# Moving the preparations of the edge messages ahead of the turned pass, and tile-wise waits for all pools, in a graph network kernel

## The chip, the cores and the metric

The kernel runs on one core of a Trainium2 chip. The core has five engines with a queue each: TensorE (PE, matmuls), VectorE (DVE), ScalarE (ACT), GpSimd (POOL) and SyncE (SP, which only issues transfers). Each works through its own instructions in a fixed order and waits for the others by semaphores. Transfers are issued by SP and ACT, and by POOL for indirect ones (gathers by an index), and run on 16 DMA engines. The metric is the device time of one execution in microseconds; three runs of the kernel before gave a median of 4243.05 us.

## The reference

There are 6,250 nodes with 64 features, 206,250 edges sorted by destination, and 64 features for each edge. Four layers follow each other, each on the normalised nodes and added to them:

```python
h = jnp.maximum(_layernorm(x, axis=-1), 0.0)
x = x + _L0_gnn_ref(h, edge_index, ...)   # two normalised sums over neighbours, W3, relu, W4
h = jnp.maximum(_layernorm(x, axis=-1), 0.0)
x = x + _L1_gnn_ref(h, edge_index)        # one sum, rows and columns exchanged
h = jnp.maximum(_layernorm(x, axis=-1), 0.0)
x = x + _L2_gnn_ref(h, edge_attr_64, ...) # messages, see below
h = jnp.maximum(_layernorm(x, axis=-1), 0.0)
x = x + _L3_gnn_ref(edge_index, h)        # three sums, averaged
```

The third one:

```python
Vp = leaky_relu(V @ pAw + pAb, 0.2) @ pBw + pBb
x = relu(relu(E @ mlp_w1 + mlp_b1) @ mlp_w2 + mlp_b2)
msg = sigmoid(x @ Bw + Bb) * Vp[src] + (x @ Cw + Cb)
M = clip(msg, 1e-5, None) ** 2
mean = segment_sum(M, dst, n) / maximum(cnt, 1.0)[:, None]
return mean ** 0.5
```

## The kernel before

The function `fast` does all of it; a second one, `general`, stands in a conditional block that is entered only if `fast` finds its assumptions on the edges broken, which these inputs don't do.

*Stages.* The nodes are padded to 49 blocks of 128, in 7 chunks of 7 blocks. The adjacency matrix A is built first, in 14 strips of 448 columns, in bf16, each written to device memory (L928 to L962); the first sum runs beside it, and its tail, `hidden`, makes V3. Then come two gathers (`gather`, L972): each multiplies all of A with the nodes, three bf16 parts of each value, strip by strip. A strip is loaded by SP in 7 pieces of 784 KB from a pool `apool` of 16 buffers, so there are 98 pieces to a gather, and one piece is 21 matmuls. After every second strip a function of chunk c runs: `convolved(c)` in the first gather, which ends in U3, the input of the second; `turned(c)` in the second (L1017), the turned pass. `turned(c)` adds to X, takes the layer norm (`normed`: DVE operations, ACT's square root at L695, DVE again), transposes on PE, multiplies by pAw, applies the leaky step `aT` on DVE (L1029), multiplies by pBw, adds the bias and stores the chunk of Vp to device memory (L1036).

*The messages.* Edges go in 202 groups of 1,024. For each group POOL issues 8 indirect fetches of rows of Vp (`fetched`, L1235, line 1238), SP loads the edge features, and PE, ACT and DVE work on groups in a pipeline written out by hand (`slot`, L1312, under `manual_schedule`). The fetch needs all 7 chunks of Vp and the indices src_g; v has 4 buffers. Beside the groups, slots take on part of the last layer's first sum and the comparison of A with its transpose (`some_of`).

*The preparations.* Before the first slot, L1050 to L1114 make what the slots need: weights on a diagonal (in the pool `const`, loaded at the start of the program), BC, the biases in three bf16 parts (a chain of five DVE operations and three small transfers on SP, BC_b), the index tables src_g and dst_g (one transfer of 808 KB each on SP, in runs of 8 integers of 4 bytes), a check that each edge lies in its window (`origin`, 194 memsets on POOL; `rel`, `off`, `missed` on DVE), `lane`, `own`, `count`. Those that are used later lie in the pool cpool, those used only here in tpool, which is closed at L1114, and mpool of the slots comes on its bytes.

*Order and memory.* Outside `slot` the order of the instructions on each engine is chosen when the program is built, by a scheduler that takes what is ready in its own model of time, earlier lines first; on the chip that order is kept. Pools are laid out as a stack from the lower end of SBUF. A pool that opens on the bytes of closed ones waits: all its tiles wait for every user of these pools. The same holds for PSUM. In the compiled program SP's and ACT's transfers share eight completion semaphores in turn, and a transfer waits for the one that had its semaphore before.

Of the kernel before, what the change touches and what calls it, by code (L numbers as in the profile page):

```python
# [8 lines left out]
F32 = mybir.dt.float32  # L9
# [9 lines left out]
D = 64  # L19
# [596 lines left out]
def fast(ctx, tc, bad, x, src, dst, edge_attr, W3, b3, W4, b4, w1, b1, w2, b2, Bw, Bb, Cw, Cb,  # L616
# [40 lines left out]
            nc.scalar.dma_start(t[k * D:(k + 1) * D, k * D:(k + 1) * D], m)  # L657
        return t

    node = ctx.enter_context(tc.tile_pool(name="node", bufs=1))  # L660
    stat = ctx.enter_context(tc.tile_pool(name="stat", bufs=2))
    deg_dst = const.tile([P, NB], F32, name="deg_dst")
    missed = const.tile([P, 3], F32, name="missed")

    def blocks(c):
        return slice(c * CB, (c + 1) * CB)

    def over_features(v, n=CB):
        return v.unsqueeze(2).to_broadcast([P, n, D])

    def over_blocks(v, n):
        return v.unsqueeze(1).to_broadcast([P, n, D])
# [71 lines left out]

    X = node.tile([P, NB, D], F32, name="X")
    nc.scalar.dma_start(X, x.rearrange("(b p) f -> p b f", p=P))
    early = ExitStack()
    early_pool = early.enter_context(tc.tile_pool(name="early_pool", bufs=1))
    with ExitStack() as ph:

        ipool = ph.enter_context(tc.tile_pool(name="ipool", bufs=1))
        with ExitStack() as first:
            dpool = first.enter_context(tc.tile_pool(name="dpool", bufs=1))
            dst_i = dpool.tile([P, K1], I32, name="dst_i")
            nc.sync.dma_start(dst_i, dst.rearrange("(p k) -> p k", p=P))
            src_i = dpool.tile([P, K1], I32, name="src_i")
# [31 lines left out]
        exact_i = ipool.tile([P, GC], I32, name="exact_i")  # L788
        junk = ipool.tile([P, P], F32, name="junk")
        looked = ExitStack()  # L790
        npool = looked.enter_context(tc.tile_pool(name="npool", bufs=1))
        near = npool.tile([P, NS], F32, name="near")
        nc.sync.dma_start(near, looks.partition_broadcast(P))
        for c in range(GC):
# [5 lines left out]
        looked.close()  # L800


        rpool = ph.enter_context(tc.tile_pool(name="rpool", bufs=3))
        opool = ph.enter_context(tc.tile_pool(name="opool", bufs=2))
        spool = ph.enter_context(tc.tile_pool(name="spool", bufs=2))
        wpool = ph.enter_context(tc.tile_pool(name="wpool", bufs=1))

        key = ipool.tile([P, 2, GC * P], BF16, name="key")
        below = ipool.tile([P, 3, GC], F32, name="below")
# [9 lines left out]

        with ExitStack() as ps:  # L820
            first = ExitStack()
            psum = first.enter_context(tc.tile_pool(name="ps_", bufs=1, space=PSUM))
            p = psum.tile([P, 512], F32, name="p_node")
            nc.tensor.transpose(p[:D, :P], W3_sb, ident)
            nc.vector.tensor_copy(W3T, p[:D, :P])
# [47 lines left out]
            nc.tensor.transpose(p[:, :NB], by_block, ident[:NB, :NB])  # L873
            nc.vector.tensor_copy(deg_dst, p[:, :NB])
            first.close()
            psum = ps.enter_context(tc.tile_pool(name="ps0", bufs=1, space=PSUM))
            norm0 = inverse_root(deg_dst, 1, "norm0")
            norm3 = inverse_root(deg_dst, 0, "norm3")

# [107 lines left out]


    with ExitStack() as ph:
        wpool = ph.enter_context(tc.tile_pool(name="wpool", bufs=2))  # L990
        U3 = of_nodes(node)
        with tc.tile_pool(name="apool", bufs=16) as apool, \
                tc.tile_pool(name="ps1", bufs=1, space=PSUM) as psum:

            def convolved(c, y):
                z = wpool.tile([P, CB, D], F32, name="z")
                nc.scalar.activation(z, y, AF.Copy)
                add_whole(z, V3, c)
                nc.vector.tensor_mul(z, z, over_features(norm0[:, blocks(c)]))
                nc.vector.tensor_add(z, z, over_blocks(b4_r, CB))  # L1000
                nc.vector.tensor_add(X[:, blocks(c), :], X[:, blocks(c), :], z)
                h = wpool.tile([P, CB, D], F32, name="h")
                normed_and_split(h, U3, c, norm3)

            gather(apool, wpool, psum, V3, convolved)

        pAw_sb = wpool.tile([D, D], F32, name="pAw_sb")
        nc.scalar.dma_start(pAw_sb, pAw)
        pBw_sb = wpool.tile([D, D], F32, name="pBw_sb")
        nc.scalar.dma_start(pBw_sb, pBw)  # L1010
        pAb_c = column(pAb, 1, "pAb_c")
        pBb_r = rows(pBb, "pBb_r")

        with tc.tile_pool(name="apool", bufs=16) as apool, \
                tc.tile_pool(name="ps2", bufs=1, space=PSUM) as psum:

            def turned(c, y):  # L1017
                z = wpool.tile([P, CB, D], F32, name="z")
                nc.vector.tensor_mul(z, y, over_features(norm3[:, blocks(c)]))
                nc.vector.tensor_add(X[:, blocks(c), :], X[:, blocks(c), :], z)  # L1020
                h = wpool.tile([P, CB, D], F32, name="h")
                normed(h, X[:, blocks(c), :])
                hT = to_features(wpool, psum, h)
                aT = wpool.tile([D, W], F32, name="aT")
                for lo, hi in ((0, 512), (512, W)):
                    p_a = psum.tile([D, 512], F32, name="p_a", bufs=2)
                    nc.tensor.matmul(p_a[:, :hi - lo], pAw_sb, hT[:, lo:hi], start=True, stop=True)
                    nc.scalar.activation(aT[:, lo:hi], p_a[:, :hi - lo], AF.Identity, bias=pAb_c)
                nc.vector.scalar_tensor_tensor(aT, aT, 0.2, aT, op0=OP.mult, op1=OP.max)  # L1029
                p_v = psum.tile([P, CB, D], F32, name="p_v", bufs=2)  # L1030
                for k in range(CB):
                    nc.tensor.matmul(p_v[:, k, :], aT[:, k * P:(k + 1) * P], pBw_sb,
                                     start=True, stop=True)
                v = wpool.tile([P, CB, D], F32, name="v")
                nc.vector.tensor_add(v, p_v, over_blocks(pBb_r, CB))
                nc.sync.dma_start(  # L1036
                    Vp_dram[c * W:(c + 1) * W, :].rearrange("(b p) f -> p b f", p=P), v)

            gather(apool, wpool, psum, U3, turned)


    early.close()
    late = ctx.enter_context(tc.tile_pool(name="late", bufs=1))
    H = late.tile([P, NB, D], F32, name="H")
    U3 = of_nodes(node)
    part = ctx.enter_context(tc.tile_pool(name="part", bufs=1))
    Y = part.tile([P, CS, CW], F32, name="Y")
    piece_pool = ctx.enter_context(tc.tile_pool(name="piece_pool", bufs=3))
    with ExitStack() as ph:
        cpool = ph.enter_context(tc.tile_pool(name="cpool", bufs=1))  # L1050
        before = ExitStack()
        tpool = before.enter_context(tc.tile_pool(name="tpool", bufs=1))
        w1_d = diagonal(w1, "w1_d")
        w2_d = diagonal(w2, "w2_d")
        b1_c = column(b1, 2, "b1_c")
# [56 lines left out]
                       allow_small_or_imprecise_dtypes=True)  # L1112

        before.close()  # L1114
        mpool = ph.enter_context(tc.tile_pool(name="mpool", bufs=3))
        ps_a = ph.enter_context(tc.tile_pool(name="ps_a", bufs=1, space=PSUM))
        n1 = stat.tile([P, NB], F32, name="n1")
        nc.vector.tensor_scalar_max(n1, deg_dst, 1.0)
        nc.vector.reciprocal(n1, n1)
# [255 lines left out]
        nc.vector.tensor_add(of_all[:, 0:1], of_all[:, 0:1], of_all[:, 2:3])  # L1375
        nc.vector.tensor_copy(bad, of_all[0:1, 0:1])


    with ExitStack() as ph:
        apool = ph.enter_context(tc.tile_pool(name="apool", bufs=12))  # L1380
        wpool = ph.enter_context(tc.tile_pool(name="wpool", bufs=2))
        psum = ph.enter_context(tc.tile_pool(name="ps4", bufs=1, space=PSUM))
        upool = ph.enter_context(tc.tile_pool(name="upool", bufs=1))

        for layer in range(3):
            V3 = of_nodes((upool, node)[layer]) if layer < 2 else None
# [77 lines left out]
```

## Time and profile before

| what | value |
|---|---|
| runs, median (lowest to highest) | 4243.05 us (4241.24 to 4245.13) |
| the profiled execution | 3727.58 us |
| its span | 3725.9 us |
| PE busy | 3092.7 us (83%) |
| POOL busy | 1666.7 us (45%) |
| DVE busy | 1890.3 us (51%) |
| ACT busy | 1282.9 us (34%) |
| read and written in device memory | 562.82 and 83.58 MB |
| first gather's first matmul | 614.14 us |
| second gather's first piece issued | 830.74 us |
| last matmul of the second gather ends | 1082.52 us |
| first fetch of the messages | 1128.00 us |

The profiled execution is 515 us shorter than the median of the runs without a profile; the trace shows only the former. Times in the profile count from the start of the span. A row of the timeline gives start, duration, engine, line, operation, output and inputs, and in brackets how long the engine had been idle and what ended that wait. `SPq`, `ACTq` and `POOLq` are the issue of transfers on these engines.

### The profile page before, as it was taken

The numbers are of one execution on the slowest core, as the hardware profiler recorded it, in microseconds if no ns is written. First come the engines' busy times: TensorE is split into PE (matmuls) and PEld (weight loads), VectorE is DVE, ScalarE is ACT, GpSimd is POOL, SyncE is SP. The second block draws the span as 40 slices with busy tenths as digits, with TensorE's granted clock in tenths as the row PEclk, the third lists the DMA queues.
The fourth block names the chain that finished last, engine by engine and source line by source line (L and its number), as shares of the span: only waits on it lengthen the run. The fifth ranks groups of instructions, "written<-read, shape, count | busy, mean of one in ns | idle before, by whom it ended". The sixth has DMA issues, their size and how long they took to land.

```text
span 3725.9 us, 57673 instructions
## 1 busy us (share of the span) xinstructions
PE 3092.7 (83%) x23299; PEld 1853.5 (50%) x23299; DVE 1890.3 (51%) x3525; ACT 1282.9 (34%) x2108; POOL 1666.7 (45%) x1870
## 2 busy tenths in 40 slices
PE   0499998999967777888878788787888887799999
PEld 0366665555544444444444444454444444466665
DVE  5999992221214555555655655555555565530100
ACT  0477772001103334433433443443443443210000
POOL 4100000000006777777777777777777777400000
PEclk9999998999987887888888888888888888899999
DMA  3244445968894333344344334334333433499997
GB/s 108 82 183 183 182 184 245 421 270 334 332 188 142 87 88 83 104 110 129 87 119 121 103 104 119 105 102 119 103 108 107 129 104 99 147 350 376 355 357 310
DMA packets 278027, 650.35 MB, mean 175 GB/s; under 512 B 106506, under 2 KB 158788, under 8 KB 275700
## 3 DMA queue, kind: packets, MB, share of 16 engines
q1 hardware_dynamic: 220036, 584.91, 43.4%
q0 software_dynamic: 54112, 58.92, 8.1%
q8 instruction: 185, 3.03, 0.3%
q10 hardware_dynamic: 3600, 2.73, 0.3%
q14 instruction: 94, 0.76, 0.1%
HBM read 562.82 MB, written 83.58 MB: 173 GB/s over the span
## 4 chain that ended last, share of the span: by engine, by line
PE 35%; POOL 32%; issue 14%; DMA 9%; DVE 8%; ACT 2%; POOLq 0%; DVEq 0%; ACTq 0%; SPq 0%
POOL v L1238 32%; PE p_sum L742 26%; DMA v<-Vp_dram,src_g 6%; PE p_a L944 3%; PE p_node L733 2%; DVE hd L935 1%; DVE lo L935 1%; PE p_bc L1264 1%; DMA dst_g<-in_dst 1%; DMA piece<-A 1%; DVE m L1273 0%; DVE m L1274 0%; PE p_node L915 0%; DVE junk L849 0%; PE p_node L725 0%
## 5 line engine op out<-in xcount | busy, mean ns | idle before, releaser
L1238 POOL DMA_INDIRECT v<-Vp_dram,src_g x1616 | 1606.2, 994 | 529.1 <-issue 460.8
L742 PE MATMUL p_sum<-piece,U 128*64 128x448 bf16 x10290 | 1051.7, 360 | 20.0 <-issue 9.9
L742 PEld LDWEIGHTS <-U 128*64 128x64 bf16 x12348 | 694.9, 111 | 527.5 <-issue 95.5
L1264 PE MATMUL p_bc<-BC,h 128*128 128x256 f32 x1616 | 603.6, 509 | 0.0
L1273 DVE TENSOR_TENSOR m<-gate,v 128x512 f32<-128x512 f32 x202 | 140.0, 693 | 798.1 <-DMA v<-Vp_dram,src_g 567.5
L1260 PE MATMUL p_bc<-BC_b,ones 3*128 3x512 bf16 x404 | 182.0, 450 | 359.4 <-DVE m L1274 358.8
L1280 ACT ACTIVATE m<-m 128x512 bf16<-128x512 f32 x202 | 127.3, 630 | 990.7 <-DVE m L1275 990.7
L1090 POOL MEMSET origin<- 128x1 f32 (+1 forms) x194 | 6.5, 96 | 970.8 <-PE p_sum L742 970.8
L1264 PEld LDWEIGHTS p_bc<-BC,h 128*128 128x128 f32 x1616 | 349.7, 240 | 157.6 <-issue 117.1
L1260 PEld LDWEIGHTS <-ones 3*128 3x128 bf16 x404 | 37.5, 93 | 613.6 <-DVE m L1274 486.2
L948 ACT ACTIVATE strip<-p_a 128x784 bf16<-128x784 f32 x392 | 301.7, 820 | 90.0 <-PE p_a L944 88.6
L1250 PE MATMUL p<-h,w_d 128*128 128x512 f32 x404 | 222.6, 633 | 50.7 <-ACT h L1254 50.7
L983 ACT ACTIVATE y<-p_sum 128x448 f32<-128x448 f32 x56 | 30.4, 543 | 678.1 <-PE p_sum L742 678.1
L1254 ACT ACTIVATE h<-p,b_c 128x512 f32<-128x512 f32 x404 | 255.0, 684 | 3.5 <-PE p L1250 3.4
L935 DVE TENSOR_TENSOR lo<-count,key 128x2048 bf16<-128x2048 bf16 x196 | 239.7, 1223 | 0.0
L742 PE MATMUL p_sum<-strip,U 128*64 128x448 bf16 x2058 | 236.2, 358 | 0.4 <-ACT strip L948 0.4
L1156 DVE SCALAR_TENSOR_TENSOR junk<-p_sum,there 128x896 bf16<-128x896 bf16 x196 | 212.3, 1083 | 12.1 <-PE p_e L1246 9.9
L944 PE MATMUL p_a<-hd,lo 128*128 128x98 bf16 x3136 | 189.5, 214 | 33.3 <-DVE lo L935 31.9
L1250 PE MATMUL p<-eT,w_d 128*128 128x512 f32 x404 | 212.3, 608 | 0.0
L944 PEld LDWEIGHTS <-lo 128*128 128x128 bf16 x3136 | 160.0, 101 | 103.4 <-DVE lo L935 81.5
L1391 DVE TENSOR_TENSOR z<-p_node,norm 128x448 f32<-128x448 f32 x21 | 13.1, 625 | 390.3 <-PE p_node L733 390.3
L1292 PE MATMUL p_s<-m,to 128*128 128x192 bf16 x1616 | 202.7, 278 | 1.1 <-DVE r_s L1300 0.4
(177 smaller groups left out, 3191.8 us busy)
## 6 DMA issues: line engine op xcount, KB each, us to landing
piece<-A SPq DMA_DIRECT2D x498, 784.0 KB, 8.7
A<-strip SPq DMA_DIRECT2D x14, 5488.0 KB, 16.5
e<-in_edge_attr SPq DMA_DIRECT2D x202, 256.0 KB, 2.8
v<-Vp_dram,src_g POOLq DMA_INDIRECT x1616
there<-A SPq DMA_DIRECT2D x56, 448.0 KB, 3.9
there<-A SPq DMA_DIRECT2D x56, 336.0 KB, 5.2
pairs<-pair SPq DMA_DIRECT2D x1, 1616.0 KB
Vp_dram<-v SPq DMA_DIRECT2D x7, 224.0 KB, 2.3
```

Of the source, the lines that this page charges most:

```text
L742: nc.tensor.matmul(p[half * D:(half + 1) * D, :w], U3[:, b, k, :], at_block, start=(i < 2), stop=(i >= 3 * n - 2))
L935: nc.vector.tensor_tensor(t, of.unsqueeze(1).to_broadcast(t.shape), key[:, k, at:at + GB].rearrange("p (h j) -> p h j", j=GQ) .unsqueeze(2 ...
L944: nc.tensor.matmul(p[:, j, :2 * NB], lo[:, g // GQ, :, g % GQ], hd[:, g // GQ, :, g % GQ], start=True, stop=True)
L948: nc.scalar.activation(strip[:, :, col:col + 2 * SG].rearrange("p b (j l) -> p b j l", l=2), p[:, :, :2 * NB].rearrange("p j (b l) -> p b ...
L1156: nc.vector.scalar_tensor_tensor(junk, p.rearrange("p a q -> p (a q)"), 0.0, there, op0=OP.add, op1=OP.not_equal, accum_out=unlike[:, n:n ...
L1238: nc.gpsimd.indirect_dma_start(out=v[:, j, :], out_offset=None, in_=Vp_dram[:, :], in_offset=bass.IndirectOffsetOnAxis(ap=src_g[:, g, j:j ...
L1250: nc.tensor.matmul(of[g][p], w, of[g].pop(x), start=True, stop=True)
L1254: nc.scalar.activation(of[g][t], of[g].pop(p), **how)
L1260: nc.tensor.matmul(p_bc[:, 4 * b:4 * b + 4].rearrange("p j o f -> p (j o f)"), ones, BC_b, start=True, stop=False)
L1264: nc.tensor.matmul(p_bc[:, 2 * q:2 * q + 2].rearrange("p j o f -> p (j o f)"), h2[:, q * P:(q + 1) * P], BC, start=False, stop=(k == 1))
L1273: nc.vector.tensor_mul(m, of[g].pop("gate"), of[g].pop("v"))
L1292: nc.tensor.matmul(p, to[:, :, j], m3[:, j].rearrange("p t f -> p (t f)"), start=(j == 0), stop=(j == J - 1))
```

## The change

All pools of `fast` get `reuse_waits="tile"`: a tile that comes on bytes of released pools waits only for the users of earlier tiles on its own bytes (in PSUM, on its own bank), not for all users of these pools. The preparations of the messages, unaltered in themselves, stand ahead of the turned pass's `apool` and PSUM pool instead of after the pass. cpool and tpool are opened with `side="right"`, at the upper end of SBUF; tpool is closed before the turned pass's `apool` opens, cpool after the messages. That `apool` has 14 buffers for 16.

```diff
-    node = ctx.enter_context(tc.tile_pool(name="node", bufs=1))
-    stat = ctx.enter_context(tc.tile_pool(name="stat", bufs=2))
+    node = ctx.enter_context(tc.tile_pool(name="node", bufs=1, reuse_waits="tile"))
+    stat = ctx.enter_context(tc.tile_pool(name="stat", bufs=2, reuse_waits="tile"))
...
+    apart = ctx.enter_context(ExitStack())
     early = ExitStack()
-    early_pool = early.enter_context(tc.tile_pool(name="early_pool", bufs=1))
+    early_pool = early.enter_context(tc.tile_pool(name="early_pool", bufs=1, reuse_waits="tile"))
...
         pBb_r = rows(pBb, "pBb_r")
 
-        with tc.tile_pool(name="apool", bufs=16) as apool, \
-                tc.tile_pool(name="ps2", bufs=1, space=PSUM) as psum:
+        cpool = apart.enter_context(tc.tile_pool(name="cpool", bufs=1, side="right", reuse_waits="tile"))
+        before = ExitStack()
+        tpool = before.enter_context(tc.tile_pool(name="tpool", bufs=1, side="right", reuse_waits="tile"))
+        w1_d = diagonal(w1, "w1_d")
...
+        BC = cpool.tile([P, 4 * D], F32, name="BC")
+        nc.vector.memset(BC, 0.0)
...
+        src_g = cpool.tile([P, G, J], I32, name="src_g")
+        nc.sync.dma_start(src_g, src.rearrange("(g p j) -> p g j", p=P, j=J))
+        dst_g = tpool.tile([P, G, J], I32, name="dst_g")
+        nc.sync.dma_start(dst_g, dst.rearrange("(g p j) -> p g j", p=P, j=J))
...
+        count = cpool.tile([P, P, J], BF16, name="count")
...
+        before.close()
+
+
+        with tc.tile_pool(name="apool", bufs=14, reuse_waits="tile") as apool, \
+                tc.tile_pool(name="ps2", bufs=1, space=PSUM, reuse_waits="tile") as psum:
...
     with ExitStack() as ph:
-        cpool = ph.enter_context(tc.tile_pool(name="cpool", bufs=1))
-        before = ExitStack()
-        tpool = before.enter_context(tc.tile_pool(name="tpool", bufs=1))
-        w1_d = diagonal(w1, "w1_d")
...
-        before.close()
-        mpool = ph.enter_context(tc.tile_pool(name="mpool", bufs=3))
-        ps_a = ph.enter_context(tc.tile_pool(name="ps_a", bufs=1, space=PSUM))
+        mpool = ph.enter_context(tc.tile_pool(name="mpool", bufs=3, reuse_waits="tile"))
+        ps_a = ph.enter_context(tc.tile_pool(name="ps_a", bufs=1, space=PSUM, reuse_waits="tile"))
...
         nc.vector.tensor_copy(bad, of_all[0:1, 0:1])
 
+    apart.close()
+
```

## The prediction

> **What bounds the kernel now.** First the forty slices of the page and its chain, then the largest group, then the timeline around the border between the turned pass and the messages.
>
> ```profile
> PE   0499998999967777888878788787888887799999
> ...
> POOL 4100000000006777777777777777777777400000
> ...
> PEclk9999998999987887888888888888888888899999
> ...
> PE 35%; POOL 32%; issue 14%; DMA 9%; DVE 8%; ACT 2%; POOLq 0%; DVEq 0%; ACTq 0%; SPq 0%
> ...
> L1238 POOL DMA_INDIRECT v<-Vp_dram,src_g x1616 | 1606.2, 994 | 529.1 <-issue 460.8
> ```
>
> The reader is to see three stretches. PE is near full from the third to the twelfth slice (building, then two gathers) and in the last five. Between, POOL has one fetch behind the other: 1616 of 994 ns with about 0.30 us between two. From the first fetch (1128.00) to the end of the last (3226.4) is 2098 us for 202 groups, 10.39 us each. Whatever lets the first fetch start earlier therefore ends the messages earlier by as much. The border:
>
> ```profile
> 1082.64 6.51 POOL L1090 MEMSET origin<- 128x3 f32 x194 [970.75 <-PE p_sum L742]
> ...
> 1088.90 8.94 SPq L1084 DMA_DIRECT2D dst_g<-in_dst  x1
> ...
> 1101.67 0.30 ACT L695 ACTIVATE v<-v,eps 128x7 f32<-128x7 f32 x1 [18.56 <-DMA bias<-in_L_gnn_Bb]
> ...
> 1115.02 1.84 DVE L1093 TENSOR_TENSOR rel<-dst_g,origin 128x1616 f32<-128x1616 int32 x1 [4.76 <-DMA dst_g<-in_dst]
> 1116.78 1.08 DVE L1029 SCALAR_TENSOR_TENSOR aT<-aT 64x896 f32<-64x896 f32 x1
> ...
> 1121.84 0.39 SPq L1036 DMA_DIRECT2D Vp_dram<-v  x1
> ...
> 1125.41 1.83 DVE L1099 TENSOR_REDUCE missed<-off 128x1 f32<-128x1616 f32 x1
> ...
> 1128.00 0.97 POOL L1238 DMA_INDIRECT v<-Vp_dram,src_g  x1 [36.96 <-DMA piece<-A]
> ```
>
> The last gather matmul ends at 1082.52; the first fetch comes 45.5 us later. In that gap the tail of turned(6) and the preparations stand in each other's way twice: ACT's square root of the norm, whose input is ready at 1088.43, runs at 1101.67 because ACT is held among the bias DMAs; and the leaky step aT, ready at 1109.41, runs at 1116.78 because `rel` is ahead of it on DVE and waits for dst_g, which takes 26.03 us. Last, the fetch's buffer lies on tpool's bytes, and tpool's last user, L1099, ends at 1127.24. The releaser printed (piece) is the last landing near it; the compiled wait lists all eight DMA semaphores and this DVE operation.
>
> The windows view of the same stretch and of the gathers (length, busy times, clock, DMA share, GB/s):
>
> ```profile
> 750.00:800.00 50.00, 49.93 (x500) 29.56 (x496) 9.52 (x18) 3.81 (x8) 0.00 (x0) 1.00 1.01 409
> 800.00:830.00 30.00, 29.93 (x302) 17.86 (x301) 8.93 (x16) 2.90 (x6) 0.00 (x0) 1.00 0.01 5
> ...
> 980.00:1030.00 50.00, 48.27 (x451) 28.31 (x449) 10.21 (x17) 6.15 (x12) 0.00 (x0) 1.00 0.76 293
> ...
> 1095.00:1100.00 5.00, 0.00 (x0) 0.00 (x0) 0.00 (x0) 0.00 (x0) 0.00 (x0) 0.50 1.36 47
> ```
>
> PE is full in the gathers; DMA is idle in the last 30 us of the convolved gather; src_g and dst_g move at some 50 GB/s against 409 for pieces.
>
> **What the Trainium skill says.** "DMA: Bandwidth & Descriptors", section "Issuing engines are not separate DMA queues": transfers from all engines run on the same 16 engines and interleave. The trace agrees: ACT's bias DMAs, a few bytes each, stop between 1087 and 1100.69 while src_g and dst_g run from SP. The same page, "Why small descriptors are slow (HBM only)", puts a fixed cost on each short descriptor; here the runs are 32 bytes (eight int32) and the rate is 35 to 70 GB/s in the 5-us windows from 1086 to 1115. "Perfetto Trace Analysis", "Identifying Dependency Chains": waits for several engines sit in extra semaphore instructions ahead; so the fetch's label is not the whole wait, as said above. "TensorE: Matmul & The Clock Gate", "Part 1": an idle PE falls to half clock; the window above shows 0.50.
>
> **The change, part by part.**
>
> *The tail of turned(6), -24 us.* With the preparations gone from the border: the square root 13.2 us earlier (1101.67 - 1088.46). The steps from there to aT's input keep their times (PE transposes, two evictions, p_a, two ACT steps: to 1109.41, now 1096.2). aT then follows at once, 7.3 us more (1116.78 - 1109.45). p_v, the addition and Vp_dram's issue keep their distance, so the issue moves from 1121.84 to 1101.3, landing (2.22) 1103.5, and the fetch 0.7 later, as before between L1099's end and it: 1104.2 for 1128.00, -23.8. What is late next is turned(6)'s own chain, 21.7 us, which stays. PE still idles there, so its clock gives little; nothing is counted.
>
> *Where the preparations go.* On the compiled layout of the kernel before, SBUF ends at 229,344 bytes and apool's 16 buffers of 6,272 lie at 115,968 to 216,320. The new cpool (15,424) and tpool (27,392) lie from 186,528 up: under buffers 11 to 15 of the convolved gather, whose last pieces PE reads between about 798 (buffer 13) and 830.7 (buffer 15). So dst_g (bytes of 12 and 13) can be loaded from about 800, into the idle DMA window; src_g, BC, `off` overlap buffer 15 and come at 830.7; bias overlaps 11 (826). The turned pass's 14 buffers end at 203,776: its buffers 11 to 13 lie on tpool and must wait for the preparations there.
>
> *The instructions moved.* POOL: 194 memsets (6.51) and the iota (1.94), where POOL has nothing else: 0. DVE: bias chain 2.59, rel 1.84, off 0.98, mask 0.98, is_lt 0.99, cast 0.99, sum 1.83, reduce 1.83: 12.0 us, in a pass in which DVE is busy 46.5 of 250 us: 0, unless one of them waits in front of convolved(6), whose result PE needs 13 us into the turned pass. ACT: 4 BC and 8 bias DMAs at 0.2 to 0.6 us, some 5 us of issue; PE needs ACT each 15 us for a PSUM eviction, with two buffers: 0 unless held as at 1087. (w_d and b_c lie in const and are loaded at the start already.) SP: three BC_b, src_g, dst_g, ahead of or among the pieces. The two big ones took 32 us together (1082.6 to 1114.9), so 16 each. Over the whole pass there is room: 80 MB in 250 us where 409 GB/s would carry 102. At the start of the pass there is none, since the prefetch is shallow then.
>
> *The turned pass's start, +12 us (from -4 to +40).* The best: pieces are prefetched through the border, nothing waits; the 2.6 us for the first piece and a little clock go: -4. My value: a reopened pool in the kernel before hands out buffer 0, then the last ones, so the second to fourth pieces lie on tpool's bytes. src_g is issued at 830.7 and runs 16 us; bias, its DVE chain and the BC_b DMAs, which queue behind src_g, end near 849, and the held pieces land at about 850 (pieces 4 us). PE read the second piece at 837.3 before; so 12.5 us late. Pieces for the other buffers are in by then, and nothing later is short. That U3's last blocks are late by ACT's wait in src_g's shadow lies within the same stall. Fourteen buffers for sixteen: 14 times 2.2 us is still 31 us of lead, 0. The worst is the rival below.
>
> *Tile waits elsewhere.* At the start, `near` waits for all of dpool, so for `pairs<-none` (27.12), though its bytes are those of dst_i and src_i, read last at 20.4. Its load can go beside pairs' store (5.27): -3 (0 to -5). First gather: pieces wait until 609.83 for the last user of wpool. PE is idle about 11 of the 21.7 us from 592.4 to 614.14. All of it, and the cold clock, would be -13; but buffers 14 and 15, second and third in that order, lie on wpool's z, free only at 609.75, so just one piece (2.2) and about 1 us of latency gain: -3. End of the messages: PE waits there for finished(6)'s chain on DVE, not for bytes: 0. The messages' rhythm, 10.39 us on POOL, is not touched: 0.
>
> Sum: -3 - 3 + 12 - 24 = -18 us. The profiled execution took 3727.58 us (span 3725.9, 1.7 around it); it would be 3710. The timed runs have a median of 4243.05, 515 us longer than the profiled one, and the profile doesn't show where. I take the 18 us over as they are: 4225. Stretched like the whole (1.14) they would be 20.
>
> **The rivals.** (1) *Everything opens.* Pieces flow through both borders, preparations cost nothing: -5 - 13 - 4 - 24 = -46, so 4197. For it: DMA idle at 800 to 830, DVE and POOL idle; against: the order in which buffers are handed out. (2) *The stall takes the gain, slower.* One mechanism: the second piece of the turned pass waits for tpool's bytes, these for DVE, DVE for dst_g, and dst_g runs together with src_g from 830.7 rather than at 800. Then 830.7 + 32 + 9.4 (rel to reduce) + 4 = 876 for a piece that was read at 837.3: +39, in all -3 - 3 + 39 - 24 = +9, so 4252, slower by the bound below; it decides from a stall of 39 us and loses all gain at 30. For it: this same pair held ACT 13 us and DVE 7 before; against: dst_g's own bytes are free at 800. (3) *It doesn't do what it says.* The preparations stay late, because their bytes or their place on the queues are still behind the turned pass; only the small borders gain: -5, so 4238. For it: the order of DVE and SP is fixed when the program is built, and it put `rel` before aT wrongly already; against: the bytes are free 250 us earlier.
>
> **How the numbers follow.** Forecast 0.50, rival 1 0.20, rival 2 0.18, rival 3 0.12. A measurement of this kernel tells about 0.2% (8.5 us) from no change. The forecast's own range is 4208 to 4238 (stall 0 to 27 us, with the small gains moving), of which some 0.04 lies within 0.2%; rival 2 has 0.02 there. So faster 0.66, same 0.18, slower 0.16. The range, leaving 0.1 out at each end: 4198 to 4253.
>
> **What would show it.** Right: the first fetch 20 to 25 us after the last matmul of the turned pass instead of 45.5; L695 of turned(6) with no wait over 1 us; dst_g issued near 800 and POOL's memsets before 1000; a PE wait for `piece` of 10 to 15 us within the first 20 us of the turned pass; 10.39 us per group after it. Wrong: a gap near 45 us still (rival 3), no PE wait at the turned pass's start and a first gather beginning near 600 (rival 1), or a PE wait over 30 us there (rival 2). A changed rhythm of the fetches, or a longer first stage, would be a cause that I haven't named.

## The result and the profile after

The changed kernel took 4248.52 us (median of 12 runs, 4220.21 to 4275.03) against 4240.1 us for the kernel before beside it (12 runs, 4229.53 to 4258.43): a ratio of 1.0011, 95% interval 0.9992 to 1.0029. The forecast was 4225. The profiled execution took 4244.66 us, its span is 4242.9 us.

The first profile of the kernel before came from an execution 515 us shorter than that kernel's timed runs. The experiments show a likely reason: chips differ. On two chips the kernel before takes 3724 and 3726 us, on another one 4246, and for the changed kernel nearly all of the difference lies in the messages (last section). On which chip the first profile was taken isn't recorded; its length and its messages (10.39 us per group) are those of the faster kind. So the borders are compared below between profiles of one kind of chip, and times only as ratios to runs of the kernel before on the same chip.

The page after, the slices of two of its rows and its largest group:

```profile
PE   0599999879756667777777777677777777789999
POOL 4000000000167656666565666565666656500000
...
L1241 POOL DMA_INDIRECT v<-Vp_dram,src_g x1616 | 1609.7, 996 | 1306.5 <-DVE m L1276 505.7
```

The ninth slice of PE, from 849 us, is no longer full: that is a new hole in PE at the start of the turned pass. POOL's fetches are as long as before (996 ns), but POOL waits between them; that belongs to the chip, not to the change (*after_again* below). The hole in the timeline (start, duration, engine, line, operation; in brackets the idle time before and what ended it):

```profile
830.44 0.39 SPq L1047 DMA_DIRECT2D src_g<-in_src  x1
...
834.48 0.28 ACTq L1031 DMA_DIRECT2D bias<-in_L_gnn_Bb  x1
...
834.93 10.52 SPq L1049 DMA_DIRECT2D dst_g<-in_dst  x1
...
848.52 0.23 ACTq L1032 DMA_DIRECT2D bias<-in_L_gnn_Cb  x1
...
850.28 0.30 ACT L695 ACTIVATE v<-v,eps 128x7 f32<-128x7 f32 x1 [17.55 <-DMA bias<-in_L_gnn_Bb]
...
855.76 6.17 SPq L1042 DMA_DIRECT2D BC_b<-bias  x3
861.98 16.77 SPq L981 DMA_DIRECT2D piece<-A  x12
862.98 1.84 DVE L1058 TENSOR_TENSOR rel<-dst_g,origin 128x1616 f32<-128x1616 int32 x1 [4.08 <-DMA dst_g<-in_dst]
866.42 4.14 PE L742 MATMUL p_sum<-piece,U 128*64 128x448 bf16 x21 [34.28 <-DMA piece<-A]
...
874.65 5.81 PE L742 MATMUL p_sum<-piece,U 128*64 128x448 bf16 x30 [4.08 <-DMA piece<-A]
```

No piece of the turned pass is issued before 861.98: src_g, dst_g and three BC_b loads stand ahead of it on SP. PE waits 34.28 and then 4.08 us, and the first 21 matmuls take 4.14 us at a granted clock of 0.54, where 21 take 2.27 at 1.00 (tile_only, at 828.34). SP's own waits there, summed by what ended them (us in total, times, longest):

```profile
SPq L1042 <- DVE bias L1039: 13.4, 1, 13.4
SPq L981 <- DVE off L1063: 7.8, 1, 7.8
SPq L981 <- DMA piece<-A: 7.8, 5, 1.6
SPq L1049 <- DMA BC<-in_L_gnn_Bw: 4.1, 1, 4.1
```

From the bottom: dst_g waits 4.1 us for a completion semaphore that it shares with one of ACT's loads, and its issue takes 10.52. BC_b waits 13.4 for the bias chain. That chain is held because ACT's bias loads stand still from 834.8 to 848.5: the next one shares its completion semaphore with src_g, whose sixteenth and last increment the trace has at 848.50. The second piece, whose buffer lies on the bytes of `off`, waits 7.8 for DVE, and DVE had waited for dst_g. The windows (length, busy times of PE, its weight loads, DVE, ACT and POOL, then clock, DMA share and GB/s) show that the idle DMA time just before the border was not used:

```profile
800.00:830.00 30.00, 29.93 (x302) 18.05 (x303) 8.97 (x16) 2.60 (x6) 7.99 (x185) 1.00 0.02 9
830.00:860.00 30.00, 1.51 (x14) 0.97 (x8) 11.04 (x28) 2.54 (x5) 0.00 (x0) 0.60 1.60 55
```

The other border, in the timeline:

```profile
1125.04 0.30 ACT L695 ACTIVATE v<-v,eps 128x7 f32<-128x7 f32 x1 [5.34 <-DVE v L694]
...
1132.82 1.08 DVE L1097 SCALAR_TENSOR_TENSOR aT<-aT 64x896 f32<-64x896 f32 x1 [6.59 <-ACT aT L1096]
...
1140.98 0.97 POOL L1241 DMA_INDIRECT v<-Vp_dram,src_g  x1 [332.99 <-DMA Vp_dram<-v]
```

The root follows its input at once, the leaky step follows ACT, and the fetch waits for the last chunk of Vp alone, 21.9 us after the last gather matmul instead of 45.5. What was gained here was lost at the other end of the same pass.

### The profile page after: what moved, and what is told of

Its sections match the earlier page's. It is cut to its first block, busy times and chain, and to the rows that moved or that the text cites. A ratio compares the mean times of both kernels' runs of the same rounds, so it can differ in the third digit from the quotient of the medians.

```text
span 4242.9 us, 57647 instructions
## 1 busy us (share of the span) xinstructions
PE 3301.5 (78%) x23299; PEld 1888.2 (45%) x23299; DVE 1915.5 (45%) x3525; ACT 1301.7 (31%) x2108; POOL 1670.1 (39%) x1870
## 4 chain that ended last, share of the span: by engine, by line
PE 58%; issue 14%; DVE 12%; another core or an unknown queue 8%; ACT 5%; DMA 3%; POOL 1%; DVEq 0%; SPq 0%; POOLq 0%; ACTq 0%
PE p_sum L742 27%; PE p_bc L1267 8%; PE p L1253 7%; PE p_s L1295 3%; PE p_a L945 3%; PE p_bc L1263 2%; PE p_sum L1153 2%; PE p_e L1249 2%; PE p_node L733 2%; DVE m L1276 1%; ACT h L1257 1%; DVE m L1277 1%; DVE hd L936 1%; DVE junk L1159 1%
## 5 line engine op out<-in xcount | busy, mean ns | idle before, releaser
L742 PE MATMUL p_sum<-piece,U 128*64 128x448 bf16 x10290 | 1122.7, 363 | 194.7 <-issue 143.4
L742 PEld LDWEIGHTS <-U 128*64 128x64 bf16 x12348 | 709.4, 111 | 747.8 <-issue 284.0
L1267 PE MATMUL p_bc<-BC,h 128*128 128x256 f32 x1616 | 558.6, 467 | 63.0 <-issue 60.6
L1267 PEld LDWEIGHTS p_bc<-BC,h 128*128 128x128 f32 x1616 | 320.9, 219 | 226.3 <-issue 197.0
L1295 PE MATMUL p_s<-m,to 128*128 128x192 bf16 x1616 | 232.7, 280 | 157.5 <-issue 140.7
L1253 PE MATMUL p<-h,w_d 128*128 128x512 f32 x404 | 269.5, 748 | 75.2 <-ACT h L1257 60.4
L1253 PE MATMUL p<-eT,w_d 128*128 128x512 f32 x404 | 267.7, 740 | 42.6 <-issue 29.3
L1295 PEld LDWEIGHTS <-to 128*128 128x128 bf16 x1616 | 177.5, 150 | 218.4 <-issue 212.2
L1283 ACT ACTIVATE m<-m 128x512 bf16<-128x512 f32 x202 | 127.2, 630 | 428.6 <-DVE m L1278 267.7
L1340 ACT ACTIVATE m<-m 128x512 bf16<-128x512 f32 x202 | 127.2, 630 | 420.7 <-DVE m L1339 243.9
L1249 PE MATMUL p_e<-ident,e 128*128 128x128 f32 x808 | 163.4, 319 | 107.1 <-issue 82.4
```

Source lines behind the costliest of these rows:

```text
L742: nc.tensor.matmul(p[half * D:(half + 1) * D, :w], U3[:, b, k, :], at_block, start=(i < 2), stop=(i >= 3 * n - 2))
L1249: nc.tensor.transpose(p[:, k * P:(k + 1) * P], e[:, k * P:(k + 1) * P], ident)
L1253: nc.tensor.matmul(of[g][p], w, of[g].pop(x), start=True, stop=True)
L1267: nc.tensor.matmul(p_bc[:, 2 * q:2 * q + 2].rearrange("p j o f -> p (j o f)"), h2[:, q * P:(q + 1) * P], BC, start=False, stop=(k == 1))
L1295: nc.tensor.matmul(p, to[:, :, j], m3[:, j].rearrange("p t f -> p (t f)"), start=(j == 0), stop=(j == J - 1))
```

## The experiments

**Theory.** The tail's 24 us are gained, and are given back at the start of the turned pass because work of the preparations stands ahead of the pieces on SP, at the one place where nothing is prefetched. **Rivals.** The tile-wise waits, or 14 buffers for 16, make the loss; the messages have become slower; the index loads cost the same wherever they run.

The ratios are to runs of the kernel before on the same chip. "PE waits" is PE's sum of waits for `piece` between 815 and 1070 us, "gap" the time from the last gather matmul's end to the first fetch. The last four rows are from chips of the other kind, where the building stage also ends 4 to 6 us later than in after_again.

| kernel | median, us (before) | ratio to before, 95% | PE waits | gap | first fetch |
|---|---|---|---|---|---|
| before_again | 3723.69 | – | 2.5 | 45.5 | 1125.8 |
| tile_only | 3702.77 (3723.92) | 0.9945, 0.9932 to 0.9959 | 1.0 | 33.5 | 1107.2 |
| moved_only | 3741.72 (3726.19) | 1.0052, 1.0039 to 1.0066 | 45.1 | 21.8 | 1143.6 |
| after_again | 3734.24 (3726.19) | 1.0023, 1.0013 to 1.0033 | 38.5 | 21.8 | 1137.5 |
| dst_first | 3716.30 (3723.92) | 0.9979, 0.9973 to 0.9986 | 22.0 | 21.8 | 1118.3 |
| inside | 3719.35 (3723.92) | 0.9989, 0.9981 to 0.9998 | 25.1 | 21.8 | 1126.1 |
| bounce_after | 3714.59 (3726.19) | 0.9970, 0.9961 to 0.9980 | 19.6 | 22.0 | 1118.0 |
| bounce_inside | 3699.50 (3726.19) | 0.9933, 0.9920 to 0.9945 | 3.5 | 21.9 | 1100.2 |
| the changed kernel, first profile | 4248.52 (4240.1) | 1.0011, 0.9992 to 1.0029 | 38.4 | 21.9 | 1141.0 |
| bcb_later2 | 4242.55 (4245.9) | 1.0011, 0.9988 to 1.0033 | 38.3 | 21.8 | 1141.4 |
| bounce_bcb2 | 4226.14 (4245.9) | 0.9959, 0.9943 to 0.9976 | 17.3 | 22.0 | 1120.9 |
| bounce_tile2 | 4212.64 (4245.9) | 0.9940, 0.9916 to 0.9964 | 1.4 | 22.1 | 1101.8 |

### The two parts of the change, apart and together

*before_again*, the kernel before unaltered:

> The kernel before, unaltered, for a profile of an ordinary execution (the first one was 515 us shorter than its timed runs). Theory (the change acts at the borders only, the messages run alike in both kernels): the border is as in the first profile of the kernel before, first fetch 45 us after the last matmul of the turned pass and PE's gap between the gathers under 5 us; the messages take about 12.9 us per group, as in the profile after, and the execution about 4240 us. Rival (the change made the messages slower, 10.39 to 12.9 us per group, and only this hides a gain): the messages stay at 10.4 us per group and the execution at about 3730.

It took 3723.69 us, at 10.36 us per group. The border is as in its first profile (45.5 us); the numbers expected for the messages were wrong, since this chip has the short ones.

*after_again*, the changed kernel on such a chip:

> The changed kernel, unaltered, on the chip on which the kernel before takes 3724 us. Theory (the change acts alike on both chips: 24 us gained at the end of the turned pass and 35 us lost at its start): PE's stall at the start of the turned pass is 31 to 37 us, the border gap about 22 us, first fetch 8 to 15 us later than the 1125.8 of the kernel before, ratio to before 1.001 to 1.004. Rival (the stall was long because the other chip is slower): stall under 25 us, first fetch at 1125 or earlier, ratio 0.996 to 1.000.

As the theory said: waits of 34.3 and 4.2 us, gap 21.8, first fetch 11.7 us later than in before_again, ratio 1.0023. The messages run at 10.38 us per group, so the change did not make them slower. That rival falls.

*tile_only*, the first part alone:

```diff
-    node = ctx.enter_context(tc.tile_pool(name="node", bufs=1))
+    node = ctx.enter_context(tc.tile_pool(name="node", bufs=1, reuse_waits="tile"))
...
```

> The pools' tile-wise waits alone; the preparations stay behind the turned pass, 16 buffers in both gathers. Theory (the loss of the change lies in the preparations' place, at the start of the turned pass): no PE stall over 5 us there, the border gap stays at 40 to 46 us, total 0 to 5 us less than before (ratio 0.999 to 1.000). Rival (tile-wise waits themselves cost, by the order in which tiles are handed out or by more waits on the queues): 5 to 15 us more than before, ratio 1.001 to 1.004, with the loss at the start of a gather or in the messages.

No stall came, as the theory said, but both its numbers were wrong: it gains 21 us at the median. The first fetch comes 18.5 us earlier than in before_again. The last gather matmul ends 6.5 us earlier (1073.7 for 1080.3): the first gather begins at 605.8 instead of 613.3, of which some is lost again to a wait for the second piece, and the pieces flow over the border between the gathers. The other 12 us come from the gap, in the timeline:

```profile
1056.28 0.46 SPq L1082 DMA_DIRECT2D src_g<-in_src  x1
...
1080.34 0.38 SPq L1084 DMA_DIRECT2D dst_g<-in_dst  x1
...
1097.27 1.84 DVE L1093 TENSOR_TENSOR rel<-dst_g,origin 128x1616 f32<-128x1616 int32 x1 [9.59 <-DMA dst_g<-in_dst]
1099.02 1.08 DVE L1029 SCALAR_TENSOR_TENSOR aT<-aT 64x896 f32<-64x896 f32 x1
...
1107.25 1.24 POOL L1238 DMA_INDIRECT v<-Vp_dram,src_g  x1 [42.98 <-issue]
```

src_g's bytes come free in the midst of the pass, and its load goes out right behind the last piece; so only dst_g is left for the gap. The leaky step is still behind `rel`, and `rel` waits for dst_g, issued 16.9 us before. dst_g itself had waited on SP for a completion semaphore that it shares with one of ACT's loads of BC, and that load goes out only at 1075.46.

*moved_only*, the second part alone (the changed kernel without `reuse_waits="tile"`):

> The preparations moved ahead of the turned pass as in the changed kernel, with 14 buffers, but all pools wait as before, for every user of the pools under them. Theory (the stall comes from the moved work that stands ahead of the pieces; tile-wise waits only let some pieces go earlier): the stall at the start of the turned pass is as long or longer, 36 to 50 us, since every piece then waits for the last operation of the temporary pool; first gather as in the kernel before; ratio to before 1.002 to 1.008. Rival (the tile-wise waits, by the order in which they hand out buffers, make the stall): stall under 20 us and ratio 0.992 to 0.998.

As the theory said, the stall is longer than in the changed kernel, one wait of 45.06 us in PE's timeline:

```profile
875.92 4.32 PE L742 MATMUL p_sum<-piece,U 128*64 128x448 bf16 x22 [45.06 <-DMA piece<-A]
```

All pieces now wait for the last operation on the temporary pool. The four kernels together: tile-wise waits bring the first fetch forward by 18.5 us without the move and by 6.1 with it; the move puts it back by 17.8 without them and by 30.2 with them. The loss is the move's.

### What the stall consists of

*dst_first* exchanges two lines of the changed kernel:

```diff
         src_g = cpool.tile([P, G, J], I32, name="src_g")
-        nc.sync.dma_start(src_g, src.rearrange("(g p j) -> p g j", p=P, j=J))
         dst_g = tpool.tile([P, G, J], I32, name="dst_g")
         nc.sync.dma_start(dst_g, dst.rearrange("(g p j) -> p g j", p=P, j=J))
+        nc.sync.dma_start(src_g, src.rearrange("(g p j) -> p g j", p=P, j=J))
```

> The changed kernel with two lines exchanged: the load of dst_g is issued before that of src_g. Theory (src_g, whose bytes come free last, held dst_g and everything behind it on SP until 830): dst_g goes out at 790 to 810 and lands before 830; ahead of the pieces only src_g's 16 us and the three small loads are left, so PE's stall at the start of the turned pass falls from 35 to 15 to 20 us and the first fetch comes at 1121 to 1126 instead of 1141; about 16 us less than the changed kernel (ratio to before 0.996 to 0.999). Rival (pieces wait for the last users of the temporary pool on VectorE, not for the queue, and the order of the two loads is without effect): stall 30 us or more, first fetch at 1135 or later.

```profile
798.58 0.39 SPq L1048 DMA_DIRECT2D dst_g<-in_dst  x1
...
828.92 0.38 SPq L1049 DMA_DIRECT2D src_g<-in_src  x1
...
844.98 32.18 SPq L981 DMA_DIRECT2D piece<-A  x22
...
849.85 30.37 PE L742 MATMUL p_sum<-piece,U 128*64 128x448 bf16 x288 [22.00 <-DMA piece<-A]
```

This timeline shows dst_g in the idle 30 us, where the prediction had put it. Two lines are worth some 16 us (0.9979 for 1.0023, of 3725). The stall that is left, 22.0, is a little more than expected: src_g's load and the bias chain stay in front.

*bounce_after* makes the index loads short. The tables are rearranged from device memory to device memory in the building stage; then src_g and dst_g are contiguous loads:

```diff
+                if s in (5, 7):
+                    with tc.issue_after(stored.ins):
+                        for t, of, at in ((dst_t, dst, 5), (src_t, src, 7)):
+                            if s == at:
+                                nc.sync.dma_start(t.rearrange("p (g j) -> p g j", j=J),
+                                                  of.rearrange("(g p j) -> p g j", p=P, j=J))
...
-        nc.sync.dma_start(src_g, src.rearrange("(g p j) -> p g j", p=P, j=J))
+        nc.sync.dma_start(src_g, src_t.rearrange("p (g j) -> p g j", j=J))
```

> The changed kernel with both index tables rearranged in device memory in the building stage, where DMA is 40% busy, so that the loads of src_g and dst_g ahead of the turned pass are contiguous, 6,464 bytes per partition. Theory (the stall is the index loads' 32-byte runs): each load takes 2 to 4 us, and of the stall of 35 us what stays is the wait of the three small bias loads for their chain on ACT and DVE, 10 to 18 us; ratio to before 0.994 to 0.998. Rival (the stall is the place on the queues and the bytes, whatever the loads take: ACT, DVE and SP wait for each other in a chain): stall 25 us or more, ratio 0.999 to 1.003.

```profile
828.15 0.32 SPq L1055 DMA_DIRECT2D src_g<-src_t  x1
828.52 0.42 SPq L1057 DMA_DIRECT2D dst_g<-dst_t  x1
838.07 6.33 SPq L1050 DMA_DIRECT2D BC_b<-bias  x3
844.46 33.59 SPq L989 DMA_DIRECT2D piece<-A  x22
848.92 4.31 PE L742 MATMUL p_sum<-piece,U 128*64 128x448 bf16 x21 [19.06 <-DMA piece<-A]
```

Half the stall goes: src_g takes 4.3 us to land, and dst_g, whose turn falls on another semaphore now, goes out at once. The building stage is as long as before (the last strip's matmuls at 575.9 us, 575.4 in after_again). ACT's bias loads now stand still for 1.6 us at most. But SP stands still from 828.9 to 838.1 and again inside BC_b, for the bias chain, and 19.06 us are left, just over the theory's 18. Something else is hidden in the first of these waits: 6.5 us of it went to a completion semaphore shared with one of ACT's loads.

*bcb_later2* takes the opposite half: the index loads stay, BC_b's loads go behind the store of chunk 1, and their sources into the pool that stays.

```diff
+                if c == 1:
+                    with tc.issue_after(kept.ins):
+                        for k in range(3):
+                            nc.sync.dma_start(BC_b[k:k + 1, :],
+                                              bias3[k].rearrange("o a b f -> o (a b f)"))
```

> The changed kernel with one part of the preparations put elsewhere: the three small loads of BC_b stand on SP behind the store of the turned pass's chunk 1 instead of ahead of the first piece (their sources lie in the pool that stays). The two index loads stay ahead of the pieces. Theory (two things follow each other in the stall of 36.4 us: the issue of the index loads, until about 842, and then SP's wait for the bias chain that BC_b needs, until 858): the pieces go out at about 842, but share the DMA engines with what is left of dst_g; stall 20 to 27 us, ratio to before 0.997 to 1.000. Rival (the DMA engines are taken by the index loads until 860 whatever SP does): stall 32 us or more, ratio 1.001 to 1.004.

```profile
846.59 53.81 SPq L981 DMA_DIRECT2D piece<-A  x22
...
865.98 4.23 PE L742 MATMUL p_sum<-piece,U 128*64 128x448 bf16 x21 [32.66 <-DMA piece<-A]
875.89 24.45 PE L742 MATMUL p_sum<-piece,U 128*64 128x448 bf16 x234 [5.68 <-DMA piece<-A]
```

Here the rival was right and the theory wrong. The first piece goes out 15.4 us earlier than in the changed kernel, and PE gets it no earlier: it lands after 19 us instead of 4, behind the index loads. The second piece still waits for `off` and so for dst_g, and is read at 875.89 (874.65 in the changed kernel). Two causes lie beside each other, and taking away BC_b alone brings nothing.

*bounce_bcb2* takes both away, with the edits of bounce_after and bcb_later2 together:

> Both causes away: the index tables rearranged in the building stage as in bounce_after, and BC_b's loads behind chunk 1's store as in bcb_later2; the other preparations stay ahead of the turned pass. Theory (the stall of bounce_after, 19 us, is SP's wait for the bias chain): the pieces go out at 829 to 831, stall 3 to 8 us, first fetch at 1100 to 1106, ratio to before 0.993 to 0.995. Rival (the pieces wait for the temporary pool's last users on DVE, which end at 849): stall 15 us or more, ratio 0.997 or more.

Again the theory's number was too small: 9.74 and 7.53 us of waits; the ratio, 0.9959, lies between theory and rival. SP's waits say for what:

```profile
SPq L989 <- DVE off L1069: 10.9, 1, 10.9
SPq L989 <- DMA BC<-in_L_gnn_Cw: 6.4, 1, 6.4
SPq L989 <- DVE lane L1075: 3.1, 1, 3.1
```

The first piece waits 6.4 us for a completion semaphore that it shares with one of ACT's loads. The second one lies on bytes of `off` and waits 10.9 for DVE, the third 3.1 for `lane`, and everything else is queued behind these on SP. So there is a third layer under the two: the waits for DVE, which are the rival's and the ones the forecast had started from, and the shared semaphore, which neither had.

### Out of the border

*inside* spreads the preparations over the turned pass, with 11 buffers, so that no piece lies on their bytes:

```diff
-        with tc.tile_pool(name="apool", bufs=14, reuse_waits="tile") as apool, \
+        with tc.tile_pool(name="apool", bufs=11, reuse_waits="tile") as apool, \
...
+                prepare(c)
```

where `prepare(c)` holds dst_g's load and what uses it for c = 1, BC and the biases for 2, src_g's load for 3.

> The changed kernel with the preparations' operations spread over the turned pass: those with dst_g after its chunk 1, the gates' weights and biases after chunk 2, src_g after chunk 3; 11 buffers for the pieces, so that none lies on the preparations' bytes. Theory (what cost 35 us was the loads' place ahead of the pieces, when no prefetch is there): no PE stall over 6 us at the start of the turned pass, the border gap stays at about 22 us, first fetch at 1105 to 1112; 28 to 35 us less than the changed kernel, ratio to before 0.993 to 0.996. Rival (wherever the index loads run they take DMA time from the pieces, and 11 buffers don't cover it): PE waits of 10 us or more in all for pieces beside the two loads, first fetch at 1118 or later.

The stall at the border is gone, and the rival's waits are there, in PE's timeline and in the windows:

```profile
912.07 10.58 PE L742 MATMUL p_sum<-piece,U 128*64 128x448 bf16 x87 [11.31 <-DMA piece<-A]
...
997.15 3.20 PE L742 MATMUL p_sum<-piece,U 128*64 128x448 bf16 x16 [12.13 <-DMA piece<-A]
```

```profile
840.00:880.00 40.00, 38.95 (x368) 23.71 (x366) 8.61 (x16) 4.25 (x8) 0.00 (x0) 1.00 0.84 347
...
898.00:915.00 17.00, 5.69 (x40) 3.49 (x38) 6.36 (x9) 0.54 (x1) 0.00 (x0) 0.64 1.36 166
...
980.00:1000.00 20.00, 7.87 (x64) 5.88 (x62) 4.74 (x9) 0.84 (x2) 0.00 (x0) 0.70 1.47 152
```

Some 18 us after each index load is issued (882.83 and 967.01) PE runs dry. Beside a load the rate falls from 347 to 166 and 152 GB/s, and dst_g, issued at 882.83, is there for `rel` only at 909.26: 26.4 us beside pieces, for 16.9 in tile_only, where no pieces run. Of these 26 us eleven buffers cover a little over half.

*bounce_inside* is the same with the rearranged tables:

> As bounce_after, and the preparations inside the turned pass (after chunks 1, 2 and 3) with 11 buffers. Theory (each of the two loads took some 25 us of the DMA engines, twice 13 us of PE waits in that place; short loads cost nothing there): no PE wait for a piece over 3 us in the turned pass, border gap 22 us, first fetch at 1093 to 1100, ratio to before 0.989 to 0.993. Rival (11 buffers are too few, or the rearranging lengthens the building stage): PE waits of 8 us or more in the turned pass, or the last strip is built over 5 us later; first fetch at 1108 or later, ratio 0.995 or more.

PE's longest wait for a piece in the pass is 2.33 us, at its start:

```profile
836.20 10.19 PE L742 MATMUL p_sum<-piece,U 128*64 128x448 bf16 x105 [2.33 <-DMA piece<-A]
```

The first fetch at 1100.2 is 25.6 us before that of before_again; the medians differ by 26.7 us, ratio 0.9933, both just past the upper end of what was expected. So eleven buffers are enough, which also answers the rival of 14 buffers for 16, and the loads' form was nearly the whole cost inside the pass (25.1 us of waits, now 3.5). Of PE's 38.5 us of waits in after_again, the place inside the pass alone takes away 13.4, the short loads alone 18.9, both together 35.0.

*bounce_tile2* leaves the preparations behind the pass and rearranges the tables:

> The pools' tile-wise waits alone (preparations behind the turned pass, 16 buffers), with the index tables rearranged in the building stage. Theory (of the 33.5 us between the last matmul of the turned pass and the first fetch in tile_only, some 10 are waits for dst_g's short runs on DVE and for semaphores on ACT): gap 23 to 27 us, first fetch at 1097 to 1101, ratio to before 0.992 to 0.994, as good as moving the preparations into the pass. Rival (the preparations' own work on DVE, 12 us, and their place ahead of the leaky step are what the gap consists of): gap 31 us or more, ratio 0.994 to 0.996.

```profile
1069.68 0.32 SPq L1092 DMA_DIRECT2D dst_g<-dst_t  x1
...
1086.69 1.83 DVE L1101 TENSOR_TENSOR rel<-dst_g,origin 128x1616 f32<-128x1616 int32 x1
...
1093.36 1.08 DVE L1037 SCALAR_TENSOR_TENSOR aT<-aT 64x896 f32<-64x896 f32 x1
...
1101.79 0.98 POOL L1246 DMA_INDIRECT v<-Vp_dram,src_g  x1 [31.60 <-DMA BC_b<-bias]
```

The gap is 22.1 us, a little better than expected and as short as with the preparations moved: `rel` and the others fit into the pauses that DVE has in turned(6)'s chain, and the leaky step follows ACT's end (1093.33) at once. So the preparations' work on DVE is not what fills the gap in tile_only; the wait for dst_g is. Two things about dst_g differ between the two kernels, though. Contiguous, it lands 5.9 us after its issue instead of 16.8. And it goes out 10.0 us before the last gather matmul ends instead of 6.6 us after it, since it waits for the semaphore of a piece now and no longer for that of ACT's load. By these figures either would be enough: an estimate has dst_g there 12.5 us after the gather with the short load alone and 6.8 with the early issue alone, where the leaky step's input was ready after 15.4 in tile_only. No run takes them apart. bounce_inside (0.9933), bounce_tile2 (0.9940) and tile_only (0.9945) lie within each other's intervals; all three beat both kernels, by 0.6 to 0.9%. That bounce_tile2 is faster than tile_only is shown by the gap, 22.1 for 33.5 us, not by the times.

## Why the prediction was right or wrong

The range held the time, but the forecast's own case did not happen: 4225 was expected and 4248.52 came, with an interval of the ratio that holds 1, where 0.66 had been given to a faster kernel. The range reached that far only because of the second rival (+9 us, 4252), and that one came almost as written: src_g and dst_g run together from 830, the second piece waits for the temporary pool's bytes, and PE reads it at 874.65, where the rival had 876. What the rival lacked is the first piece, which waits 34.28 us behind BC_b on SP. It doesn't add to the sum: with BC_b out of the way (bcb_later2) PE waits 38.3 us all the same.

- *The tail of turned(6), -24:* right. The gap went from 45.5 to 21.8 us, -23.7, and what is late next is the chain named, 21.7 us.
- *Start and first gather, -3 and -3:* half. Between before_again and after_again the first gather begins 7.7 us earlier, stops once for its second piece, and ends about 3.1 us earlier, 1.2 of them from the building stage (last strip's matmuls 575.4 for 576.6; kernels with tile-wise waits differ by 2 us there). At the start the load of `near` was to go out beside the store of `pairs` at about 20, since its bytes are free. It went at 26.21 for 26.94: on SP it stands behind another store, `pairs<-none` at 25.82. That is the mistake of the next point on a small scale.
- *The start of the turned pass, +12:* this term failed. PE's waits rose from 2.5 to 38.5 us, +36.0, and a cold first piece added about 1.9 (4.14 for 2.27 us). The reason in the working: "dst_g (bytes of 12 and 13) can be loaded from about 800". Its bytes were free, its place on SP was not: src_g stands in front, and src_g's bytes come free last. dst_first shows the size of that assumption: with the two lines exchanged dst_g does go out at 798.58, and PE's waits fall by 16.5 us. The second assumption, that the first pieces are prefetched while only those on the temporary pool's bytes are held, fell too: on SP every piece is behind BC_b, and BC_b behind the bias chain.
- *A reading in the working:* the prediction took it as agreeing with the shared DMA engines that ACT's bias loads stop until 1100.69 while src_g and dst_g run. The trace of the kernel before shows another reason: that load shares a completion semaphore with src_g, whose last increment comes at 1100.67. So ACT waited for src_g itself, and when src_g moved, the hold moved with it.
- *The sum:* -3.1 + 36.0 + 1.9 - 23.7 is +11.1 us; the first fetch came 11.7 us later, the two profiled executions differ by 11.3 (3735.02 and 3723.69, two chips of one kind), and the medians by 8.1 on the one chip (ratio 1.0023).
- *The messages' rhythm, 0:* right; 10.36 and 10.38 us per group on one kind of chip. Taking the 18 us over as they are, unstretched, was right as well: on the other kind of chip the borders keep their lengths (38.4 for 38.5, 21.9 for 21.8) while the execution takes 514 us more (4248.52 for 3734.24).
- *Tile waits as a whole, -6:* near what they bring beside the move (6.1 us at the first fetch, from moved_only to after_again). That they are worth 21 us alone, 12 of them because src_g's load leaves the gap, was not seen, and the move hid it.
- *The signs to look for:* the fetch at 21.9 us and the memsets at 799.59: as foretold. L695 waits 5.34 us instead of under 1, but for its own input alone. dst_g near 800 and a PE wait of 10 to 15 us: not; "a PE wait over 30 us" had been put down as the sign of the second rival.

## What to carry to other kernels

A transfer starts when its bytes are free and its place on the issuing queue has come: before counting on idle DMA time, write down what stands in front of it and when that can go. Work that is taken out of one gap should not go to the head of a queue at another gap; put it where prefetch is deep, and keep it short there as well (in *inside* the long loads still cost 25.1 us of waits). And look first at the form of a load that won't fit: two tables in runs of 32 bytes were a large part of the wait at both ends, and with tables made contiguous in the building stage, where DMA had time to spare (share 0.40), the wait in the gap was gone without moving anything, though the order of the semaphores had a part in that which was not measured.

## What the hardware showed that was not expected

- *Chips differ by some 515 us, nearly all of it in the messages.* In the chip with the long time, PE starts some matmuls and their weight loads 0.70 or 1.41 us after the ones before, though nothing in the profile holds them ("issue" in the brackets), as in these rows of the changed kernel's timeline:

```profile
2008.66 0.55 PE L742 MATMUL p_sum<-piece,U 128*64 128x448 bf16 x3 [1.04 <-issue]
2010.07 0.35 PE L742 MATMUL p_sum<-piece,U 128*64 128x448 bf16 x1 [0.87 <-issue]
2010.80 1.23 PE L742 MATMUL p_sum<-piece,U 128*64 128x448 bf16 x3 [0.37 <-issue]
```

  From 1150 us to the last fetch the changed kernel's first profile has 498 distances between weight loads within 0.03 us of 0.70, 1.41 or 2.11 (573 us, the distances added up); after_again has 9, before_again 4. The messages take 2583 us in the one and 2097 in the other, what follows them 519 and 499, and the gathers show almost none of it. In the messages the granted clock is lower too, 0.76 for 0.86, and PE is busy for 199 us longer. Whether that is a cause or a consequence, and what makes PE wait there, stays open.
- *A slow load can hold another engine's queue through a completion semaphore.* ACT's bias load at 848.52, 256 bytes long, waits 13.8 us for src_g, a load of SP with which it shares nothing but the semaphore; src_g's last increment comes at 848.50. It works the other way round too: SP waited 4.1 us in the changed kernel, 6.4 us in bounce_bcb2 and 23.5 us in tile_only for a load of ACT. In bounce_tile2, with two transfers more in the building stage, dst_g has a piece for a partner instead. With the short loads of bounce_after ACT's longest hold is 1.6 us. The Trainium skill, "DMA: Bandwidth & Descriptors", section "Why small descriptors are slow (HBM only)", gives a fixed cost per descriptor as the reason why a load of many short runs is slow; the runs here agree with it: the same 808 KB of dst_g land after 16.8 us in runs of 32 bytes (tile_only) and after 5.9 us when they lie contiguous (bounce_tile2).
